# Attention's products turned by block reads and VectorE, and a three-pass rounding of the gate and up weights

## The chip, the cores and the metric

The kernel runs on one core of one Trainium2 chip. The metric is device time in microseconds (us) of one execution. A core has a matrix engine (TensorE, PE in the profile; its weight loads are PEld), VectorE (DVE), ScalarE (ACT), GpSimd (POOL), and SyncE (SP), which here only issues DMA transfers. Each engine takes its instructions in order; engines wait for one another by semaphores. On-chip data lies in SBUF (128 partitions), matmul results in PSUM.

## What is computed

One pre-norm block in float32 on x of shape 4 x 512 x 512: an attention of the Fourier kind, then a gated feed-forward whose weights are rounded to float8 (e4m3) values first.

```python
# attention on the layer-normed x; B=4, S=512, D=512, 16 heads of 32
q  = (x @ W_q.T ).reshape(B, S, H, hd)
kv = (x @ W_kv.T).reshape(B, S, H, hd)
qf  = l2_normalize(fft(q));  kvf = l2_normalize(fft(kv))
kvf = cumsum(kvf, axis=1)
values = ifft(qf * kvf).real.reshape(B, S, D)
x = x + values @ W_o.T
# feed-forward on the layer-normed x; I=1536
wq(w) = w.astype(float8_e4m3fn).astype(float32)
gate = silu((xn @ wq(gate_w)) * gate_scale)
up   = (xn @ wq(up_w)) * up_scale
x = x + ((gate * up) @ wq(down_w)) * down_scale
```

## The kernel before

**Tiling.** The 4 x 512 tokens are 16 chunks of 128 tokens, four to a batch entry. `x` comes in twice, plain (`load_x`) and turned (`load_xT`). The Fourier transform is folded into W_q and W_kv at the start (`fold_in`, `folded`), its inverse into W_o (`fold_out`).

**Order.** The schedule is written by hand: the order of the calls is the order on each engine. A pass `for i in range(2, N)` runs the rounds of attention. In round i chunk i is projected to its spectrum (`spectrum(i, 1)` for the keys, `spectrum(i, 0)` for the queries, eight matmuls' rows each), its squares are taken on ACT and summed on DVE (`squared`, `summed`), and `norms` raises them to -1/2 on POOL. Chunk i-1 is scaled on DVE (`k_scaled` with the carried row of the chunk before, split into `kh` by ACT and `kl` by `k_low`; `q_scaled`), summed along the tokens by two matmuls with a triangular matrix (`running`, tile `cum`), its last row is carried on (`carry`: ACT copies 32 rows to `end`, a DMA on ACT's queue takes one of them to `row`), and multiplied (`products` on DVE, `combined` on POOL). Chunk i-2 is turned by four PE transposes into PSUM and copied to `qvT` by ACT (`v_transpose`), and projected by W_o (`project`, tile `po`). Chunk i-3 gets its residual on DVE and goes to DRAM (`finish`, tensor `y_all`). `x_stats` and `x_row`, `x_center` take the mean of the next chunks' tokens out of x.

**Rounding of the weights.** 18 units of 128 x 1024 weights (two each of gate, up, down for each of three column or row blocks) are rounded to float8 values by `quant_abs` (ACT: |w| scaled down), `quant_step` (DVE: exponent mask; then an operation that makes a large value where the weight overflows, on ACT in the rounds, on POOL later), `quant_floor`, `quant_add` and `quant_sub` (DVE). These are cut into `parts`, and `next_parts(n)` issues the next n of them: at three places before the rounds, at up to three places of each round by the list `given` (42 parts), the other 27 in the first steps of the feed-forward.

**Feed-forward.** For each batch entry 12 steps of `inner` (16 matmuls `gu` of gate and up, then Silu on ACT, `f` and `fl` on DVE, `fh` on ACT) and `down` of the step before (eight matmuls `pd`). The normed tokens of entry 0 are turned by PE (`y_transpose`); those of entries 1 to 3 by `y_blocks`, which writes them to DRAM and reads them back in four DMAs of 32 x 32 blocks, and `y_turn`, which turns each block by one DVE transpose. `behind` and `between` place that work after the matmuls of a step.

**SP's queue** carries, in the order of the program, loads of x, xT and weights (`load_unit`, 1 MB each), stores of y, the loads of y for each batch entry (`load_y`), the blocks and the output.

Of the kernel before, what the change touches and what calls it, by code (L numbers as in the profile page):

```python
# [7 lines left out]
F32 = mybir.dt.float32  # L8
# [7 lines left out]
P = 128  # L16
# [5 lines left out]

E4M3_MIN_NORMAL = 2.0**-6
E4M3_OVERFLOW = 464.0
ROUNDER = 1.5 * 2.0**20
DOWN = 2.0**-40
HUGE = 2.0**127
# [3 lines left out]
def tile_fft_attention_then_fp8_ffn(  # L31
# [53 lines left out]

    chunks = [(b, c) for b in range(B) for c in range(TC)]
# [13 lines left out]
    def load_x(i):  # L100
        b, c = chunks[i]
        t = work.tile([P, D], F32, tag="x", name=f"x_{b}_{c}", bufs=6)
        nc.sync.dma_start(t, x[b, c * P : (c + 1) * P, :])
        xt[i] = t
# [23 lines left out]
    nc.gpsimd.memset(over, -E4M3_OVERFLOW * DOWN * HUGE)  # L128

# [11 lines left out]
    xn_all = dram.tile([B, TC, P, D], F32, name="xn_all")  # L141

# [53 lines left out]
    def quant_abs(u):  # L196
        k = units[u][3]
        w = staged[u][:, k : k + QH, :]
        a = work.tile([P, QH, D], F32, tag="qa", name=f"qa_{u}")
        nc.scalar.activation(a, w, AF.Abs, scale=DOWN)  # L200
        quant[u] = (w, a)

    def quant_step(u, in_rounds):
        w, a = quant[u]
        m = work.tile([P, QH, D], F32, tag="qm", name=f"qm_{u}")
        nc.vector.tensor_scalar(
            m.bitcast(I32), a.bitcast(I32), 0x7F800000, None, ALU.bitwise_and
        )
        if in_rounds:
            nc.scalar.activation(a, a, AF.Identity, scale=HUGE, bias=over)  # L210
        else:
            nc.gpsimd.tensor_scalar(a, a, -E4M3_OVERFLOW * DOWN, HUGE, ALU.add, ALU.mult)
        quant[u] = (w, a, m)

    def quant_floor(u):
        _, a, m = quant[u]
        nc.vector.scalar_tensor_tensor(m, a, E4M3_MIN_NORMAL * DOWN, m, ALU.max, ALU.max)  # L217

    def quant_add(u):
        w, a, m = quant[u]  # L220
        nc.vector.scalar_tensor_tensor(a, m, ROUNDER / DOWN, w, ALU.mult, ALU.add)  # L221

    def quant_sub(u):
        _, a, m = quant[u]
        nc.vector.scalar_tensor_tensor(units[u][0], m, -ROUNDER / DOWN, a, ALU.mult, ALU.add)
# [4 lines left out]
    for u in range(len(units)):  # L230
        parts += [(quant_floor, u), (quant_add, u)]
        if u + 1 < len(units):
            parts.append((quant_step, u + 1))
        parts.append((quant_sub, u))

    def next_parts(n, in_rounds=False):

        for f, u in parts[:n]:
            if f is quant_step:
                f(u, in_rounds)  # L240
                if in_rounds and units[u][3] == 0 and u + QH < U1:
                    load_unit(u + QH)
            else:
                f(u)
            if f is quant_add and u + 1 < len(units):
                quant_abs(u + 1)
        del parts[:n]


    def stats(src, name):  # L250

        less = work.tile([P, 1], F32, tag="less", name=f"less_{name}", bufs=4)
        rstd = work.tile([P, 1], F32, tag="dev", name=f"dev_{name}", bufs=6)
        each = work.tile([P, D], F32, tag="end", name=f"each_{name}", bufs=1)
        nc.scalar.activation(each, src, AF.Identity, accum_out=less)
        nc.scalar.activation(less, less, AF.Copy, scale=-1.0 / D)
        nc.scalar.activation(each, src, AF.Square, bias=less, accum_out=rstd)
        nc.scalar.activation(rstd, rstd, AF.Identity, scale=1.0 / D, bias=eps)
        nc.gpsimd.tensor_tensor(rstd, rstd, nhalf[:, 0:1], ALU.pow)
        return less, rstd  # L260
# [12 lines left out]

    def heads(t):
        return t.rearrange("p (h f) -> p h f", f=HD)


    st_x, rows, xns, pqs, sss, rns, qns, kns, carries, cums, qvs, qvTs, pos = (
        {} for _ in range(13)
    )  # L280

    def nm(i):
        return "%d_%d" % chunks[i]

    def x_stats(i):
        st_x[i] = stats(xt[i], nm(i))
# [20 lines left out]
    def squares(i, j):  # L307
        squared(i, j)
        summed(i, j)
# [59 lines left out]
    def products(i):  # L369

        qn, cum = qns.pop(i), cums.pop(i)
        qv = work.tile([P, D], F32, tag="qv", name=f"qv_{nm(i)}")
        cross = work.tile([P, D], F32, tag="cross", name=f"cross_{nm(i)}", bufs=1)
        qh, ch, xh = heads(qn), heads(cum), heads(cross)
        nc.vector.tensor_tensor(qv, qn, cum, ALU.mult)
        nc.vector.tensor_tensor(xh[:, :, :HK], qh[:, :, :HK], ch[:, :, HK:], ALU.mult)
        nc.vector.tensor_tensor(xh[:, :, HK:], qh[:, :, HK:], ch[:, :, :HK], ALU.mult)
        qvs[i] = (qv, cross)
# [9 lines left out]
    def v_transpose(i):  # L388
        pt = transpose(qvs.pop(i)[0], f"v{nm(i)}")
        qvTs[i] = work.tile([P, KC, P], F32, tag="qvT", name=f"qvT_{nm(i)}", bufs=1)  # L390
        nc.scalar.copy(qvTs[i], pt)
# [25 lines left out]

    def y_norm(b, c):
        xns["y", b, c] = normed(ys[b][:, c, :], st_y.pop((b, c)), f"f{b}_{c}")
# [11 lines left out]
    def y_blocks(b, c):  # L431

        nc.sync.dma_start(xn_all[b, c], xns.pop(("y", b, c)))
        src = xn_all[b, c].rearrange("(i t) (k j f) -> j t k i f", t=HD, j=P // HD, f=HD)
        z = work.tile([P, KC, P], F32, tag="x", name=f"z_{b}_{c}", bufs=6)
        for j in range(P // HD):
            nc.sync.dma_start(
                z[j * HD : (j + 1) * HD].rearrange("t k (i f) -> t k i f", f=HD), src[j]
            )
        xns["z", b, c] = z  # L440

    def y_turn(b, c):
        if c == 0:
            yhs[b] = big_tile(f"yh_{b}", F32R)
            yls[b] = big_tile(f"yl_{b}", F32R)
        z = xns.pop(("z", b, c))
        t = work.tile([P, KC, P], F32, tag="xT", name=f"t_{b}_{c}", bufs=3)
        nc.vector.transpose(t.rearrange("p k n -> p (k n)"), z.rearrange("p k n -> p (k n)"))
        s = slice(c * P, (c + 1) * P)
        hi, lo = yhs[b][:, :, s], yls[b][:, :, s]  # L450
        nc.scalar.copy(hi, t)
        nc.gpsimd.tensor_tensor(lo, t, hi.bitcast(F32), ALU.subtract)
# [5 lines left out]
    def inner(n, on_pe, between):  # L458
# [19 lines left out]
        nc.vector.scalar_tensor_tensor(f, pgu[1], gus[:, 1, m : m + 1], g, ALU.mult, ALU.mult)  # L478
        fh = work.tile([P, S], F32R, tag="kh", name=f"fh_{b}_{m}", bufs=3)
# [7 lines left out]
    def down(steps):  # L487
# [17 lines left out]
        if steps[-1] % MC == MC - 1:  # L505
            for c in range(TC):
                o = work.tile([P, D], F32, tag="x", name=f"o_{b}_{c}", bufs=6)
                nc.vector.tensor_tensor(o, pds[b][c], dsc, ALU.mult)  # L508
                add = nc.vector if b == B - 1 and c % 2 else nc.gpsimd
                add.tensor_tensor(o, o, ys[b][:, c, :], ALU.add)  # L510
                nc.sync.dma_start(out[b, c * P : (c + 1) * P, :], o)
# [49 lines left out]
    next_parts(1, True)  # L561
# [9 lines left out]
    squares(1, 1)  # L571
    norms(1, 1)
    x_row(2)
    x_center(2)
    q_scaled(0)
    products(0)
    combined(0)
    spectrum(1, 0)
    squares(1, 0)
    k_scaled(1)  # L580
    k_low(1)
    norms(1, 0)


    given = [4 if i in (2, 5, 7, 9, 11) else 3 for i in range(N - 3)] + [2, 2, 0]
    for i in range(2, N):
        spectrum(i, 1)
        if i == N - 6:
            load_y(0)
        at(load_xT, i + 2)  # L590
        if i > 2:
            k_scaled(i - 1)
            finish(i - 3)
        at(load_x, i + 2)
        if i > 2:
            k_low(i - 1)
        squared(i, 1)
        v_transpose(i - 2)
        if i == 2:
            x_stats(3)  # L600
        next_parts(given[i] // 3, True)
        if i > 2:
            q_scaled(i - 1)
        summed(i, 1)
        norms(i, 1)
        if i == 2:
            q_scaled(1)
# [10 lines left out]
        combined(i - 1)  # L618
        if i == N - 1:
            y_transpose(0, TC - 2)  # L620
            y_transpose(0, TC - 1)
# [6 lines left out]
        project(i - 2)  # L628
# [6 lines left out]
    for _, u in parts:  # L635
        if u not in staged:
            load_unit(u)
            if 1 not in ys:
                load_y(1)
    finish(N - 3)  # L640
# [4 lines left out]
    def on_pe(n, part):  # L645
        if part == 0 and n < 2:
            v_transpose(N - 2 + n)
            if n == 1:
                finish(N - 2)
        elif part == 1 and n == 0:  # L650
            running(N - 1)
            products(N - 1)
            combined(N - 1)
            project(N - 2, "tp")
# [5 lines left out]
    def behind(n):  # L660
        b, m = divmod(n, MC)
        if n == 1:
            project(N - 1, "tp")
            finish(N - 1)
# [10 lines left out]
        if b + 1 < B and 0 <= m - 3 < TC:  # L675
            y_stats(b + 1, m - 3)


    for n in range(STEPS + 1):
        if n < STEPS:  # L680
            inner(n, on_pe, between)
# [70 lines left out]
```

## Time and profile before

The unprofiled runs took 479.96, 481.14 and 481.37 us, with a median of 481.14. The profiled execution took 480.92; its span, from the first to the last instruction, is 479.1.

| | |
|---|---|
| median of the runs | 481.14 us |
| profiled execution, and its span | 480.92 us, 479.1 us |
| start to the first round (i = 2) on PE | 0 to 32.8 us |
| rounds 2 to 15 | 32.8 to 194.8 us |
| feed-forward, 48 steps | 194.8 to 473.4 us |
| granted TensorE clock | 0.999 |
| four PE transposes of a chunk's products | 0.27 us each, 64 in all |
| POOL's power, `rn` | 3.38 us each, 32 in all |
| bytes moved | 40.7 MB, mean 85 GB/s |

The rows of a timeline give start, duration, engine, line, operation, tiles and shapes, and in brackets the idle time before and what ended it. A row with a count (x8) merges as many instructions. The rows of a table of windows give for each stretch its length, the busy time (and count) of PE, PEld, DVE, ACT and POOL, the granted clock, the DMA engines' mean busy share and GB/s.

### The profile page before, as it was taken

To read this page: it belongs to the slowest core of one execution; us is meant where nothing else is said; L and a number is where in the kernel's file an instruction comes from. 1 tells how busy PE (TensorE), PEld (TensorE's weight loads), DVE (VectorE), ACT (ScalarE), POOL (GpSimd) and SP (SyncE) were. 2 spreads that over 40 slices of the span, in tenths; PEclk is the share of its full clock that TensorE was granted. 3 is DMA by queue.
4 is the path that set the end of the run, shared out by engine and by line. 5 is a ranking of instruction groups with operands and counts; after the bars stand their busy time and mean duration, and the time that the engine had idled before them with its cause. 6 is when DMAs were issued, how large, how long until landed. Compare 5 with 4: busy or idle time off the path is not lost.

```text
span 479.1 us, 5013 instructions
## 1 busy us (share of the span) xinstructions
PE 466.3 (97%) x1736; PEld 313.7 (65%) x1736; DVE 286.4 (60%) x399; ACT 214.9 (45%) x418; POOL 200.9 (42%) x134
## 2 busy tenths in 40 slices
PE   6999999999999999999999999999999999999995
PEld 5534454444444445568888888888888888888883
DVE  1558998888998787768898352333433332522225
ACT  3647475655646864315753325533226433222220
POOL 0257999987897986531332140122210021400002
PEclk9999999999999999999999999999999999999999
DMA  8920424342442101424241040430041420200002
GB/s 288 349 66 23 154 86 134 110 148 87 140 154 68 64 22 35 164 91 150 55 100 22 1 175 2 100 77 0 22 155 36 96 46 0 89 0 1 0 0 88
DMA packets 46152, 40.72 MB, mean 85 GB/s; under 512 B 27696, under 2 KB 28080, under 8 KB 46128
## 3 DMA queue, kind: packets, MB, share of 16 engines
q1 hardware_dynamic: 45744, 40.39, 26.9%
q8 instruction: 13, 0.21, 0.2%
q14 instruction: 11, 0.09, 0.1%
q10 hardware_dynamic: 384, 0.03, 0.1%
HBM read 28.85 MB, written 11.53 MB: 84 GB/s over the span
## 4 chain that ended last, share of the span: by engine, by line
PE 77%; DVE 8%; ACT 5%; POOL 4%; DMA 3%; issue 2%; SPq 0%; DVEq 0%; ACTq 0%
PE gu L465 37%; PE pd L498 19%; PE pq L302 12%; PE po L397 6%; POOL rn L323 3%; DMA row<-end 2%; PE pkv L150 1%; PE pt_v L271 1%; ACT sq L313 1%; ACT end L364 1%; DVE ss L318 1%; DVE qm L217 1%; PE pw L165 1%; PE cum L357 1%; DVE qa L221 1%
## 5 line engine op out<-in xcount | busy, mean ns | idle before, releaser
L323 POOL TENSOR_TENSOR rn<-ss,nhalf 128x16 f32<-128x16 f32 x32 | 108.2, 3383 | 22.5 <-DVE ss L318 22.5
L478 DVE SCALAR_TENSOR_TENSOR f<-gu,gus,g 128x512 f32<-128x512 f32 x48 | 36.0, 750 | 114.4 <-PE gu L465 112.9
L465 PE MATMUL gu<-yh,wg 128*128 128x512 f32 x192 | 77.0, 401 | 0.0
L465 PE MATMUL gu<-yh,wu 128*128 128x512 f32 x192 | 76.2, 397 | 0.0
L465 PE MATMUL gu<-yl,wg 128*128 128x512 f32 x192 | 75.8, 395 | 0.0
L498 PE MATMUL pd<-wd,fl 128*128 128x512 f32 x192 | 75.7, 394 | 0.0
L498 PE MATMUL pd<-wd,fh 128*128 128x512 f32 x192 | 75.7, 394 | 0.0
L465 PE MATMUL gu<-yl,wu 128*128 128x512 f32 x192 | 75.7, 394 | 0.0
L481 ACT CAST fh<-f 128x512 fp32r<-128x512 f32 x48 | 29.8, 621 | 90.8 <-DVE f L478 90.8
L302 PE MATMUL pq<-wkv,xT 128*128 128x512 f32 x128 | 57.7, 594 | 0.8 <-DVE xT L294 0.8
L476 ACT ACTIVATE g<-gu,gus 128x512 f32<-128x512 f32 x48 | 33.0, 688 | 55.2 <-PE gu L465 55.2
L397 PE MATMUL po<-wo,qvT 128*128 128x512 f32 x128 | 57.6, 593 | 0.0
L302 PE MATMUL pq<-wq,xT 128*128 128x512 f32 x128 | 57.6, 592 | 0.0
L510 POOL TENSOR_TENSOR o<-o,ys 128x512 f32<-128x512 f32 x14 | 17.7, 1295 | 83.6 <-DVE o L508 83.6
L483 DVE TENSOR_TENSOR fl<-f,fh 128x512 fp32r<-128x512 f32 x48 | 36.2, 755 | 27.0 <-ACT fh L481 26.8
L302 PEld LDWEIGHTS pq<-wkv,xT 128*128 128x128 f32 x128 | 24.1, 190 | 30.6 <-issue 27.5
L465 PEld LDWEIGHTS gu<-yh,wg 128*128 128x128 f32 x192 | 36.0, 188 | 9.3 <-issue 0.5
L465 PEld LDWEIGHTS gu<-yl,wg 128*128 128x128 f32 x192 | 36.0, 188 | 9.2 <-issue 0.5
L498 PEld LDWEIGHTS pd<-wd,fh 128*128 128x128 f32 x192 | 36.0, 188 | 8.9
L498 PEld LDWEIGHTS pd<-wd,fl 128*128 128x128 f32 x192 | 36.0, 188 | 8.8 <-DVE fl L483 0.2
L465 PEld LDWEIGHTS gu<-yl,wu 128*128 128x128 f32 x192 | 36.1, 188 | 8.7
L465 PEld LDWEIGHTS gu<-yh,wu 128*128 128x128 f32 x192 | 36.0, 188 | 8.5
(84 smaller groups left out, 596.4 us busy)
## 6 DMA issues: line engine op xcount, KB each, us to landing
x<-in_x SPq DMA_DIRECT2D x16, 256.0 KB, 2.8
xT<-in_xT SPq DMA_DIRECT2D x16, 256.0 KB, 2.6
y_all<-x SPq DMA_DIRECT2D x16, 256.0 KB, 2.0
ys<-y_all SPq DMA_DIRECT2D x4, 1024.0 KB, 6.8
out<-o SPq DMA_DIRECT2D x16, 256.0 KB, 2.0
rawf<-in_gate_w SPq DMA_DIRECT2D x3, 1024.0 KB, 6.9
rawf<-in_up_w SPq DMA_DIRECT2D x3, 1024.0 KB, 5.4
rawf<-in_down_w SPq DMA_DIRECT2D x3, 1024.0 KB, 6.2
```

The costliest lines, as they stand in the source:

```text
L150: nc.tensor.matmul(pw[i][:, j * P : (j + 1) * P], lhsT=r[:, j, i * P : (i + 1) * P], rhs=fwd, start=True, stop=True,)
L165: nc.tensor.matmul(pw, lhsT=inv, rhs=r[:, j, :], start=True, stop=True)
L302: nc.tensor.matmul(pq, lhsT=xTs[i][:, k, :], rhs=w[:, k, :], start=k == 0, stop=k == KC - 1)
L323: nc.gpsimd.tensor_tensor(rns[i, j], sss.pop((i, j)), nhalf, ALU.pow)
L397: nc.tensor.matmul(po, lhsT=qvT[:, k, :], rhs=wo[:, k, :], start=k == 0, stop=k == KC - 1)
L465: nc.tensor.matmul(p, lhsT=w[:, k, m * P : (m + 1) * P], rhs=v[:, k, :], start=k == 0 and v is yhs[b], stop=k == KC - 1 and v is yls[b],)
L476: nc.scalar.activation(g, pgu[0], AF.Silu, scale=gus[:, 0, m : m + 1])
L478: nc.vector.scalar_tensor_tensor(f, pgu[1], gus[:, 1, m : m + 1], g, ALU.mult, ALU.mult)
L481: nc.scalar.copy(fh, f)
L483: nc.vector.tensor_tensor(fl, f, fh.bitcast(F32), ALU.subtract)
L498: nc.tensor.matmul(pds[b][c], lhsT=v[:, c * P : (c + 1) * P], rhs=wd[:, m, :], start=m == 0 and v is fused[n][0], stop=m == MC - 1 and v i ...
L510: add.tensor_tensor(o, o, ys[b][:, c, :], ALU.add)
```

## The change

There are four parts.

1. The products `qv` are no longer turned by PE. `v_blocks` writes them to a DRAM tensor `qv_all` and reads them back in four block DMAs into `z`, all on SP's queue; `v_turn` turns the blocks with one DVE transpose into `qvT`. The helpers `blocks` and `turned` are shared with the feed-forward's `y_blocks` and `y_turn`.
2. The output projection comes a round later: round i now has `project(i - 3)`, then `v_turn(i - 2)`, and `finish(i - 4)`. Round 2 is written out ahead of the loop, which begins at 3. The last projections lie in the feed-forward's first steps. Seven x tiles for six.
3. Gate and up weights are rounded in three DVE passes: a mask that also sets a bit (`quant_step`), add, subtract. What the floor did is done by a column `c` of one number per row: ACT sums Relu of the scaled |w| beyond the overflow bound over the row, and a 128 x 1 operation makes of it the least rounder, or a huge one for a row with overflow. Down weights keep four passes. The list `given` falls to 2 or 3 a round (29 parts), six parts lie before, 25 in the feed-forward.
4. Smaller: the two half products into `cross` become one with a reversed stride; `stats` is cut into `mean` and `deviation` and writes to the tag `tmp` where it wrote to `end`; weight loads are noted in `wanted` and issued after `v_blocks`; the loads of the last weight units are spread over the feed-forward's first steps; the feed-forward's means are taken ahead of `fh` on ACT; `qv` has one buffer.

```diff
     def quant_abs(u):
+        _, src, _, k = units[u]
         w = staged[u][:, k : k + QH, :]
         a = work.tile([P, QH, D], F32, tag="qa", name=f"qa_{u}")
-        nc.scalar.activation(a, w, AF.Abs, scale=DOWN)
-        quant[u] = (w, a)
+        m = work.tile([P, QH, D], F32, tag="qm", name=f"qm_{u}")
+        c = None
+        if src is down_w:
+            nc.scalar.activation(a, w, AF.Abs, scale=DOWN)
+        else:
+            c = work.tile([P, 1], F32, tag="qc", name=f"qc_{u}")
+            nc.scalar.activation(a, w, AF.Abs, scale=UP)
+            nc.scalar.activation(m, a, AF.Relu, scale=FAR, bias=far, accum_out=c)
+            nc.scalar.activation(c, c, AF.Identity, scale=HUGE, bias=least)
+        quant[u] = (w, a, m, c)
     def quant_step(u, in_rounds):
+        if c is not None:
+            nc.vector.tensor_scalar(
+                m.bitcast(I32), a.bitcast(I32), 0x7F800000, 0x00400000, ALU.bitwise_and, ALU.bitwise_or
+            )
+            return
     def quant_add(u):
+        if c is not None:
+            nc.vector.scalar_tensor_tensor(a, m, c, w, ALU.max, ALU.add)
     def quant_sub(u):
+        if c is not None:
+            nc.vector.scalar_tensor_tensor(to, m, c, a, ALU.max, ALU.subtract, reverse1=True)
...
-        each = work.tile([P, D], F32, tag="end", name=f"each_{name}", bufs=1)
+        each = work.tile([P, D], F32, tag="tmp", name=f"each_{name}")
...
+    def blocks(z, there, tokens):
+        nc.sync.dma_start(there, tokens)
+        src = there.rearrange("(i t) (k j f) -> j t k i f", t=HD, j=P // HD, f=HD)
+        for j in range(P // HD):
+            nc.sync.dma_start(
+                z[j * HD : (j + 1) * HD].rearrange("t k (i f) -> t k i f", f=HD), src[j]
+            )
+    def turned(t, z):
+        nc.vector.transpose(t.rearrange("p k n -> p (k n)"), z.rearrange("p k n -> p (k n)"))
...
-        nc.vector.tensor_tensor(xh[:, :, :HK], qh[:, :, :HK], ch[:, :, HK:], ALU.mult)
-        nc.vector.tensor_tensor(xh[:, :, HK:], qh[:, :, HK:], ch[:, :, :HK], ALU.mult)
+        nc.vector.tensor_tensor(xh, qh, ch[:, :, ::-1, :], ALU.mult)
...
-    def v_transpose(i):
-        pt = transpose(qvs.pop(i)[0], f"v{nm(i)}")
+    def v_blocks(i):
+        zs[i] = work.tile([P, KC, P], F32, tag="z", name=f"zv_{nm(i)}", bufs=1)
+        blocks(zs[i], qv_all[i], qvs.pop(i)[0])
+    def v_turn(i):
         qvTs[i] = work.tile([P, KC, P], F32, tag="qvT", name=f"qvT_{nm(i)}", bufs=1)
-        nc.scalar.copy(qvTs[i], pt)
+        turned(qvTs[i], zs.pop(i))
...
+    load_xT(4)
+    load_x(4)
+    spectrum(2, 1)
+    squared(2, 1)
+    x_stats(3)
+    next_parts(1, True)
+    spectrum(2, 0)
+    x_row(3)
+    running(1)
+    squared(2, 0)
+    carry(1)
+    x_center(3)
+    summed(2, 1)
+    norms(2, 1)
+    q_scaled(1)
+    products(1)
+    combined(1)
+    v_blocks(1)
+    next_parts(1, True)
+    summed(2, 0)
+    norms(2, 0)
+    x_stats(4)
+    next_parts(1, True)
+    v_turn(0)
-    given = [4 if i in (2, 5, 7, 9, 11) else 3 for i in range(N - 3)] + [2, 2, 0]
-    for i in range(2, N):
+    given = [3 if i % 2 else 2 for i in range(N - 3)] + [2, 2, 0]
+    for i in range(3, N):
         spectrum(i, 1)
         at(load_xT, i + 2)
-            finish(i - 3)
+        at(finish, i - 4)
         at(load_x, i + 2)
         squared(i, 1)
-        v_transpose(i - 2)
...
         products(i - 1)
         combined(i - 1)
+        v_blocks(i - 1)
+        while wanted:
+            load_unit(wanted.pop())
...
-        project(i - 2)
+        project(i - 3)
+        v_turn(i - 2)
...
+    load_unit(U1)
+    load_y(1)
+    finish(N - 4)
...
     def on_pe(n, part):
-        if part == 0 and n < 2:
-            v_transpose(N - 2 + n)
-            if n == 1:
-                finish(N - 2)
-        elif part == 1 and n == 0:
+        if part == 1 and n == 0:
             running(N - 1)
             products(N - 1)
             combined(N - 1)
-            project(N - 2, "tp")
+            v_blocks(N - 1)
+            project(N - 3, "tp")
...
     def behind(n):
         if n == 1:
+            load_unit(U1 + QH)
+            finish(N - 3)
+            v_turn(N - 2)
+        elif n == 2:
+            project(N - 2, "tp")
+            v_turn(N - 1)
+        elif n == 3:
+            finish(N - 2)
             project(N - 1, "tp")
+            load_unit(U1 + 2 * QH)
+        elif n == 4:
             finish(N - 1)
```

## The prediction

> **What bounds the kernel now.** I read the busy shares, the chain that ended last, TensorE's (PE's) rows in order of time, a table of busy time by round, and then the other engines' rows in the same stretches.
>
> ```profile
> PE 466.3 (97%) x1736; PEld 313.7 (65%) x1736; DVE 286.4 (60%) x399; ACT 214.9 (45%) x418; POOL 200.9 (42%) x134
> ...
> PE 77%; DVE 8%; ACT 5%; POOL 4%; DMA 3%; issue 2%; SPq 0%; DVEq 0%; ACTq 0%
> ```
>
> PE is busy 97% of the span, but ends of matmuls are modelled, so the starts decide. One round of attention:
>
> ```profile
> 101.83 3.60 PE L302 MATMUL pq<-wkv,xT 128*128 128x512 f32 x8
> 105.26 0.60 PE L271 MATMUL pt_v<-tab,qv 128*128 128x128 f32 x4
> 105.70 3.60 PE L302 MATMUL pq<-wq,xT 128*128 128x512 f32 x8
> 109.14 0.27 PE L290 MATMUL row<-tab,less 128*128 128x128 f32 x1
> 109.16 0.48 PE L357 MATMUL cum<-kh,tri_r 128*128 128x512 f32 x1
> 109.48 0.40 PE L357 MATMUL cum<-kl,tri_r 128*128 128x512 f32 x1
> 109.72 3.60 PE L397 MATMUL po<-wo,qvT 128*128 128x512 f32 x8
> 113.15 3.60 PE L302 MATMUL pq<-wkv,xT 128*128 128x512 f32 x8
> ```
>
> The round starts at 101.83 and the next at 113.15, no row waits: 11.32 us of back-to-back work. The transposes cost the start of the next product less a plain product: (105.70 - 101.83) - (101.83 - 98.40) = 3.87 - 3.43 = 0.44. The feed-forward part is as dense: its steps come every 5.59 us (gu rows of the chain at 214.26, 219.85, 225.44), to 460. What the change does there beside PE is therefore free while fl comes within a step. So the rounds decide, and there the other engines are near PE (columns: PE, PEld, DVE, ACT, POOL busy):
>
> ```profile
> 75.92:87.24 11.32, 11.32 (x32) 5.39 (x32) 10.86 (x15) 6.97 (x14) 10.33 (x6) 1.00 0.25 76
> 87.24:98.56 11.32, 11.32 (x32) 5.38 (x32) 9.94 (x15) 6.01 (x13) 10.33 (x6) 1.00 0.44 151
> ...
> sum 113.40, PE 113.40 PEld 53.55 DVE 98.72 ACT 72.06 POOL 98.19; mean PE 11.34 PEld 5.35 DVE 9.87 ACT 7.21 POOL 9.82
> ```
>
> Over ten rounds VectorE (DVE) takes 9.87 and GpSimd (POOL) 9.82 of 11.34.
>
> **Part 1: transposes off PE.** Sixteen groups of four go: 14 in the rounds and 2 in the feed-forward's first steps (there 197.09 to 197.44 plus a slower next matmul, also about 0.44). 16 x 0.44 = **-7.0 us**. ScalarE (ACT) loses 16 copies of qvT at 0.58, off the path. One PE wait in front of a transpose goes as well, 0.59 at 186.54 (for DVE yl): **-0.6**.
>
> What takes their place, per chunk: a store on SP, four block reads on SP, one DVE transpose. Rows: t<-z transpose 0.70; the reads in the feed-forward: store issued at 232.26, first read at 235.16, four issues 2.71 together, last landing 2.5 after its issue. The last issue starts near 237.2, so z is there at 239.7: **7.5 us from store to z**. GpSimd ends combined() at 148.30 where the next round starts at 147.11, so z is there 1.2 + 7.5 = 8.7 us into that round. v_turn waits anyway until project() has read the one qvT buffer, at the round's end, 10.88. Cover: 2.2 us. If it is gone, DVE stands still, and behind v_turn stand k_scaled, finish, k_low, q_scaled and x_center, for which the next spectrum waits. SP's queue: per round 0.33 + 2.0 wait + 2.7 + xT 0.33 + y 0.33 + x 0.38 + at most one weight load 0.4 = 6.5 of 10.9, so x and xT come some 4 us later than now; both are wanted a round later (x by x_stats, xT by x_center), with landings of 2.8 and 2.6. No cost.
>
> A rule speaks against the reads: the Trainium skill, "DMA: Bandwidth & Descriptors", Specifications, wants 512 bytes or more per transfer, below which the engines read, modify and write; the blocks are read in 128-byte pieces. If each piece cost as one of 512, four reads would weigh like one 1 MB load, and by an estimate from that z would come some 4 to 5 us later, the case of rival 2; the trace's 2.5 us for 64 KB says no, though with less other traffic than the rounds have.
>
> **Part 2: DVE and ACT in a round.** DVE gains 0.70 (turn) and changes two cross products (0.33 apart each, 0.66) for one over 512 elements: nearest row qv, 0.60 apart; bounds 0.60 and 0.70, nothing. Gate and up units drop the floor pass (1.24). The two-operation mask, the max-with-column add and subtract are not in the trace: between their present rows (0.68, 1.22, 1.22) and those under GpSimd's shadow (1.22, 1.60, 1.72); I take the present. The rounds are given 2.5 parts each, 3.3 before: 0.8 x 1.17 = -0.95. DVE: 9.87 + 0.70 - 0.95 = **9.6 of 10.88**. ACT: per gate or up unit Relu with a sum (L210's 1.15 + 0.19) and one 128x1 row (0.30) for L210's 1.15: +0.5; minus 0.58 per round. And the step in which ACT waited for DVE (qa L210 <- qm, 14.0 us in all) goes for these units. POOL keeps its 9.82, 90% of a round: the thinnest cover. Its loop is rn(q) to q_scaled, ss, rn(k), two combined() rows, rn(q):
>
> ```profile
> 70.39 2.91 POOL L323 TENSOR_TENSOR rn<-ss,nhalf 128x16 f32<-128x16 f32 x1
> 73.26 0.56 POOL L259 TENSOR_TENSOR dev<-dev,nhalf 128x1 f32<-128x1 f32 x1
> 74.75 3.82 POOL L323 TENSOR_TENSOR rn<-ss,nhalf 128x16 f32<-128x16 f32 x1 [0.93 <-DVE ss L318]
> 78.54 0.70 POOL L385 TENSOR_TENSOR qv<-qv 128x240 f32<-128x240 f32 x1
> 79.31 1.03 POOL L386 TENSOR_TENSOR qv<-cross 128x240 f32<-128x240 f32 x1
> 80.31 3.88 POOL L323 TENSOR_TENSOR rn<-ss,nhalf 128x16 f32<-128x16 f32 x1
> ```
>
> From 70.39 to 80.31 that is 9.9 us; other turns take 10.3 to 11.8 (80.31 to 92.09), because the same operation takes 2.91 beside some DVE work and 3.88 beside other. The removed floor is such neighbour work; I take 10.4, under 10.88, cost nothing, and 11.3 as the far end (rival 1).
>
> **Part 3: the start.** Projection comes a round later, so PE has 3.43 us less to do while the first chunks pass DVE, ACT and POOL, and it waits for them. I walked rounds 2 to 4 with the rows' durations.
> - Gain: stats no longer write the tile end, so ACT does not wait for the row's DMA (13.8 us in five waits, the first 25.80 to 27.63), and x_center(2) stands ahead of summed(1,1). spectrum(2,1) starts at 31.8 for 32.79; PE waits of 0.31 and 0.39 go.
> - k_scaled(1) 36.0, kh 37.3, x_stats(3), row(3) 39.1, x_center(3) 40.1: round 3 starts on PE at 40.1 and its two spectra end at 47.0.
> - The squaring of x(3) now uses a tmp buffer that summed(2,1) must have read (40.7), so ACT reaches carry(1) at 42.6, products(1) ends at 44.4, then add, sum, step, turn to 47.5, k_scaled(2) with its row 48.8, kh 49.4, kl(2) **50.1**. cum(2) waits on PE from 47.2 to 50.1.
> - project(0) ends at 54.1; x_center(4), behind rn(2,0) at 51.2, at 54.3; round 4 starts at 54.4, round 5 at 65.4 without a wait (x_center(5) at 64.4).
>
> Before, round 5 started at 67.87. Without project's 3.43 and three transposes (1.3) that would be 63.1; I get 65.4: **+2.3 us**. Bounds: nothing, or the 3.43 that were moved.
>
> **Part 4: into the feed-forward.** cum(15) now waits 1.08 for the bank that ACT frees late, because kh waits for a row that took 6.1 us behind two 1 MB loads (issued at 189.41 and 190.64, the row at 191.96). These loads now stand behind v_blocks(14) on SP, so the row goes first (1.7): a wait of 0.3 is left, **-0.8**. The late projections (3 x 3.43) are the same work at another place. v_turn(14) stands about 13 us after the first gu row, z(14) is there at 7; for chunk 15 some 18 against 15 to 18 behind the 2 MB: no more than a DVE wait inside a step. Parts left: 25 for 27, three passes for most.
>
> **Sum**: span 479.1 - 7.0 - 0.6 + 2.3 - 0.8 = 473.0. The profiled run took 480.92, 1.8 above its span and 0.2 below the median of 481.14. 473.0 + 1.8 = 474.8, with the 0.2: **475.0**.
>
> **Rivals.** Differences under 0.3% (1.4 us) cannot be told from no change.
> 1. DVE, POOL and ACT set the round, which stays at 11.3: the 6.2 us of the 14 round transposes are not had, the rest is: 475.0 + 0.42 x 12 = **480**. For: POOL at 90%, loops of 10.3 to 11.8 now. Against: the floor and the ACT waits go. 20%.
> 2. The block reads come late in the rounds, which carry more traffic (150 GB/s in every other round against 60 in the feed-forward). The loop combined, store to z, turn, k_scaled to products, combined spans two rounds: z time + 0.6 + 7.4 + 0.6 + 2.1. With 21.8 for two rounds it decides from a z time of 11 us. With landings like the 1 MB loads (6.9 for 2.5) and 0.9 more on the store it is 12.8: 0.85 more a round, 11 rounds, **484**, slower. Against: x and xT land in 2.6 to 2.8 in the rounds. 11%.
> 3. Relu makes ACT load tables. The trace has one load of 1.28 for all its functions, and Relu is not among them. Two loads for each of 12 units are 31 us on ACT, 2.1 a round, on 7.3: it fits, but kh and the carry come 2.6 later in such rounds: about **479**. 3%. The Trainium skill, "ScalarE: Activation LUTs", Table sets, counts relu among the cheap functions that are in every set, so no load; no row here shows it.
>
> My forecast, PE setting the pace of nearly every round: 60%, 472.8 to 477.5. Another 6% for slower by something unnamed. Low end 472.8 (start free of cost); the high end reaches over rival 1 to 482.0, leaving out rival 2, the unnamed and a little below. Faster: 60 + 12 of rival 1 + 2 = 74%; same 9%; slower 17%.
>
> **What would show it.** Right: rounds 10.9 apart on PE from the fifth on, no pt_v rows, one PE wait near 2.9 at cum(2), one table load, feed-forward steps of 5.59. Wrong: rounds at 11.3 with PE waiting for x_center or cum (rival 1); DVE t<-z waiting for DMA (rival 2); or PE waits at project().

## The result, and the profile after

| | before | after |
|---|---|---|
| median of the runs | 480.97 us (479.96 to 481.37, 4 runs) | 489.09 us (488.21 to 489.91, 4 runs) |
| span of the profiled execution | 479.1 us | 486.8 us |
| round 5 begins on PE | 67.87 us | 64.72 us |
| feed-forward begins on PE | 194.81 us | 200.10 us |

The changed kernel takes 1.0172 times as long, with an interval of 1.0145 to 1.0198. It was forecast to be faster. The start is 3.2 us earlier than before, as it should be; between round 5 and the feed-forward everything is lost, and more.

The page of the kernel after: the busy shares, the chain that ended last, and the DMA issues with their median time to landing in the last column.

```profile
PE 465.5 (96%) x1672; PEld 308.6 (63%) x1672; DVE 276.8 (57%) x387; ACT 214.9 (44%) x429; POOL 191.4 (39%) x133
...
PE 63%; DVE 5%; ACT 4%; DMA 4%; issue 1%; SPq 1%; POOL 1%; DVEq 0%; ACTq 0%; POOLq 0%
...
x<-in_x SPq DMA_DIRECT2D x16, 256.0 KB, 4.9
xT<-in_xT SPq DMA_DIRECT2D x16, 256.0 KB, 4.7
qv_all<-qv SPq DMA_DIRECT2D x16, 256.0 KB, 2.0
zv<-qv_all SPq DMA_DIRECT2D x64, 64.0 KB, 2.5
```

PE has 64 instructions less (the transposes), but its share of the chain falls from 77% to 63%: it now waits for others. The block reads land in 2.5 us, as the row of the feed-forward promised; it is x and xT that land late, in 4.9 and 4.7 us where it was 2.8 and 2.6. The rows of the kernel before for these two, and for ACT's wait for x:

```profile
x<-in_x SPq DMA_DIRECT2D x16, 256.0 KB, 2.8
xT<-in_xT SPq DMA_DIRECT2D x16, 256.0 KB, 2.6
...
ACT each L255 <- DMA x<-in_x: 5.5, 2, 3.3
```

The waits of the kernel after (engine, line waited at, what ended the wait: total us, times, longest us) say whom that hits:

```profile
PE cum L413 <- ACT kh L399: 7.9, 7, 2.1
PE cum L413 <- DVE kl L404: 1.4, 6, 0.2
PE cum L413 <- ACT g L535: 0.3, 1, 0.3
...
ACT each L288 <- DMA x<-in_x: 32.3, 10, 6.8
...
ACT qa L215 <- DMA rawf<-in_down_w: 9.8, 2, 7.3
...
SPq L320 <- POOL qv L441: 71.1, 15, 6.8
SPq L323 <- DMA qv_all<-qv: 34.3, 16, 5.9
```

ACT waited for x 5.5 us in two waits before; now it is 32.3 us in ten. PE had no wait for kh before; now it has seven. SP stands 71.1 us at the block store for GpSimd's end of the products, and 34.3 us at the reads for the store to land. What follows on SP in the program waits too. A wait of the kind seen here, in PE's rows of two rounds (start, duration, and in brackets the idle time before and what ended it):

```profile
113.62 3.60 PE L358 MATMUL pq<-wkv,xT 128*128 128x512 f32 x8
...
120.49 0.27 PE L346 MATMUL row<-tab,less 128*128 128x128 f32 x1
120.52 0.48 PE L413 MATMUL cum<-kh,tri_r 128*128 128x512 f32 x1
120.84 0.40 PE L413 MATMUL cum<-kl,tri_r 128*128 128x512 f32 x1
...
124.50 3.60 PE L358 MATMUL pq<-wkv,xT 128*128 128x512 f32 x8
...
131.37 0.27 PE L346 MATMUL row<-tab,less 128*128 128x128 f32 x1
132.61 0.50 PE L413 MATMUL cum<-kh,tri_r 128*128 128x512 f32 x1 [0.96 <-ACT kh L399]
133.33 0.50 PE L413 MATMUL cum<-kl,tri_r 128*128 128x512 f32 x1 [0.23 <-DVE kl L404]
...
137.10 1.45 PE L358 MATMUL pq<-wkv,xT 128*128 128x512 f32 x3
```

The first of these rounds takes 124.50 - 113.62 = 10.88 us, exactly what was forecast. The second takes 137.10 - 124.50 = 12.60. A listed wait of 0.96 cost 1.72: kh starts 1.24 after row instead of 0.03, and kl 0.72 after kh instead of 0.32, because it is made of kh. Now ACT beside it, and below it SP, on which each row is the issue of a transfer:

```profile
123.17 0.50 ACTq L422 DMA_DIRECT2D row<-end  x1
129.92 0.63 ACT L288 ACTIVATE each<-x 128x512 f32<-128x512 f32 x1 [6.77 <-DMA x<-in_x]
...
131.95 0.60 ACT L399 CAST kh<-kn 128x512 fp32r<-128x512 f32 x1
```

```profile
106.88 0.33 SPq L320 DMA_DIRECT2D qv_all<-qv  x1
108.94 2.61 SPq L323 DMA_DIRECT2D zv<-qv_all  x4
111.64 0.57 SPq L105 DMA_DIRECT2D xT<-in_xT  x1
112.31 0.38 SPq L464 DMA_DIRECT2D y_all<-x  x1
112.74 0.42 SPq L110 DMA_DIRECT2D x<-in_x  x1
117.11 0.33 SPq L320 DMA_DIRECT2D qv_all<-qv  x1
119.17 2.60 SPq L323 DMA_DIRECT2D zv<-qv_all  x4
121.87 0.57 SPq L205 DMA_DIRECT2D rawf<-in_up_w  x1
122.54 0.45 SPq L105 DMA_DIRECT2D xT<-in_xT  x1
123.04 0.42 SPq L464 DMA_DIRECT2D y_all<-x  x1
123.51 0.67 SPq L110 DMA_DIRECT2D x<-in_x  x1
```

Read the last row first. The x load at 123.51 belongs to the round that began at 113.62; it stands behind the store, the 2 us wait for its landing, the four reads, a 1 MB load of weights, xT and y. ACT wants that x from 123.2 on, for `x_stats(i + 2)`, which is the last of the same round. It gets it at 129.92. `kh` of the next round stands behind `x_stats` on ACT, so it starts at 131.95, and PE waits. One round earlier there was no weight load in front: x was issued at 112.74, landed in 3.3 us and not in 6.3, ACT waited 5.70 us for it, and PE did not wait. What decides is not the length of ACT's wait but when `x_stats` begins: 116.19 is 2.57 us into the next round and early enough for that round's `kh`, 129.92 is 5.42 us into it and too late. In the kernel before, SP's row for x is this:

```profile
105.95 0.38 SPq L103 DMA_DIRECT2D x<-in_x  x1
```

Its round began at 101.83, so x was issued 4.12 us into it. After, it is 112.74 - 102.64 = 10.10 us into the round. Of the ten rounds from 64.72 to 188.86 in the kernel after, four take 10.87 to 10.98 us and six take 12.30 to 15.95. In the four, `x_stats` begins 0.6 to 2.6 us into the round, in the six 4.9 to 6.2 us into it. In three of the six ACT waits last for an x behind a 1 MB load (of weights twice, of y once), in two for a load of down weights and then for x, and in the last, round 14, for DVE (run 5 shows this wait).

### The profile page after: what moved, and what is told of

It reads as the page before. It is cut to its first block, busy times and chain, and to the rows that moved or that the text cites. A ratio compares the mean times of both kernels' runs of the same rounds, so it can differ in the third digit from the quotient of the medians.

```text
span 486.8 us, 5056 instructions
## 1 busy us (share of the span) xinstructions
PE 465.5 (96%) x1672; PEld 308.6 (63%) x1672; DVE 276.8 (57%) x387; ACT 214.9 (44%) x429; POOL 191.4 (39%) x133
## 2 busy tenths in 40 slices
DMA packets 82250, 49.13 MB, mean 101 GB/s; under 512 B 61744, under 2 KB 62128, under 8 KB 82224
## 4 chain that ended last, share of the span: by engine, by line
PE 63%; DVE 5%; ACT 4%; DMA 4%; issue 1%; SPq 1%; POOL 1%; DVEq 0%; ACTq 0%; POOLq 0%
PE gu L524 36%; PE pd L558 18%; PE po L455 4%; DMA x<-in_x 3%; PE pq L358 3%; ACT kh L399 1%; PE cum L413 1%; ACT sq L369 1%; SPq L323 1%; ACT each L296 1%; DVE qa L245 0%; DVE ss L374 0%; ACT each L288 0%; DVE kl L404 0%; DVE kn L396 0%
## 5 line engine op out<-in xcount | busy, mean ns | idle before, releaser
L379 POOL TENSOR_TENSOR rn<-ss,nhalf 128x16 f32<-128x16 f32 x32 | 105.0, 3281 | 25.8 <-DVE ss L374 25.8
L524 PE MATMUL gu<-yh,wg 128*128 128x512 f32 x192 | 78.0, 406 | 0.0
L455 PE MATMUL po<-wo,qvT 128*128 128x512 f32 x128 | 58.6, 601 | 0.0
L358 PEld LDWEIGHTS pq<-wq,xT 128*128 128x128 f32 x128 | 24.2, 190 | 30.4 <-issue 30.1
L298 POOL TENSOR_TENSOR dev_f<-dev_f,nhalf 128x1 f32<-128x1 f32 x16 | 10.3, 646 | 84.6 <-ACT dev_f L297 84.5
```

What stands on the lines that cost most here:

```text
L358: nc.tensor.matmul(pq, lhsT=xTs[i][:, k, :], rhs=w[:, k, :], start=k == 0, stop=k == KC - 1)
L379: nc.gpsimd.tensor_tensor(rns[i, j], sss.pop((i, j)), nhalf, ALU.pow)
L455: nc.tensor.matmul(po, lhsT=qvT[:, k, :], rhs=wo[:, k, :], start=k == 0, stop=k == KC - 1)
L524: nc.tensor.matmul(p, lhsT=w[:, k, m * P : (m + 1) * P], rhs=v[:, k, :], start=k == 0 and v is yhs[b], stop=k == KC - 1 and v is yls[b],)
```

## The experiments

The theory: x and the weights come late because of their place on SP behind the block store and reads; the transposition by blocks itself, the three-pass rounding and the later projection do what was forecast. Rivals: the block traffic (49.13 MB for 40.7) slows the other transfers wherever they stand; or another part of the change costs the time. Runs 1 to 4 were made together, 5 to 8, and 9 to 11; the median of the kernel before beside them is 480.7 us for the first two groups and 481.0 for the third.

**1. x a round earlier.** The carried row stays in its tile to make room for an eighth x tile.

```diff
-    XB = 7
+    XB = 8
...
-            row = work.tile([1, D], F32, tag="row", name=f"row_{nm(i)}", bufs=1)
+            row = end[:1, :]
...
+    load_x(5)
...
-        at(load_x, i + 2)
+        at(load_x, i + 3)
```

> The changed kernel, with each x chunk loaded one round earlier (eight x tiles; the carried row is kept in the first partition of the tile it comes from, to make room). Theory A (SP's queue: the x load stands behind the block reads and weight loads, ACT waits for it and takes kh late, PE waits at cum): ACT's waits for x fall from 32.3 us to under 3, the PE waits for kh from 7.9 us to under 2, rounds 10.9 us apart; 475 to 479 us. Rival B (the block reads' traffic slows every transfer): the waits move to the weight loads and the carried row, 483 to 488. Rival C (the loop of GpSimd, VectorE and ScalarE sets the round at 11.3 or more): ACT no longer waits for x, PE still waits at cum, 482 to 487.

481.07 us (480.16 to 482.22); against the kernel before 1.0009 [0.9996, 1.0022]. 8 us of the loss are gone, though not one byte moves less: it is the time of x that cost them. The gain falls 2 us short of theory A's range, though rounds 6 to 12 are 10.88 us each. The waits of this kernel:

```profile
PE cum L413 <- ACT kh L399: 4.2, 4, 2.1
...
ACT qa L215 <- DMA rawf<-in_down_w: 11.5, 2, 7.2
ACT each L288 <- DMA x<-in_x: 6.5, 3, 3.7
```

x is awaited about as little as before the change (6.5 us for 5.5). What is left are two waits of ACT for down weights, which also stand behind the reads on SP; `kh` is again queued behind them. Half of PE's 4.2 us, the longest wait, is in round 14.

**2. Weight loads behind x.** They are issued after x's load of the next round instead of straight after the reads.

```diff
         at(load_x, i + 2)
+        while wanted:
+            load_unit(wanted.pop())
         k_low(i - 1)
...
         v_blocks(i - 1)
-        while wanted:
-            load_unit(wanted.pop())
```

> The changed kernel, with the 1 MB weight loads issued behind the next round's x load instead of ahead of it. Theory A: in the four or five rounds that load weights x lands in about 4.5 us for 6.5 and about 2 us earlier; each such round gets 1 to 2 us shorter, 481 to 486; more waits of ACT for the weights take a part back. Rivals B and C: no gain, 487 to 490.

480.86 us (479.41 to 482.5); 1.0003 [0.9986, 1.0021]. x is issued about 1 us earlier (8.99 us into a round for 10.10) and lands without a 1 MB load in front, in 3.7 us (median) for 4.9:

```profile
PE cum L413 <- ACT kh L399: 4.3, 3, 2.2
...
ACT each L288 <- DMA x<-in_x: 28.6, 10, 4.6
```

ACT still waits 28.6 us in ten waits, but the longest is 4.6 where it was 6.8, and most of PE's waits are gone: rounds 5 to 13, from 69.25 to 167.32, take 10.86 to 11.04 us each, with `x_stats` beginning 0.8 to 3.9 us into them. So the late place of x alone costs these rounds nothing; it did so together with a 1 MB load in front. And the sum of ACT's waits is no measure of the loss; what counts is how many of them make `kh` late. What is left is lost in round 14 and in round 4, which takes 15.08: the carried row, issued 1.9 us after a load of weights, lands in 6.7 us there, and the clock falls (last section). The time lies just under theory A's range.

**3. Turned by PE again,** with the rest of the change.

```diff
     def v_blocks(i):
-        zs[i] = work.tile([P, KC, P], F32, tag="z", name=f"zv_{nm(i)}", bufs=1)
-        blocks(zs[i], qv_all[i], qvs.pop(i)[0])
+        pass
     def v_turn(i):
+        pt = transpose(qvs.pop(i)[0], f"v{nm(i)}")
...
-        turned(qvTs[i], zs.pop(i))
+        nc.scalar.copy(qvTs[i], pt)
```

> The changed kernel, with the products turned by TensorE again (no store, no block reads; one buffer more for qv), the later projection and the three-pass rounding kept. Theory A: without the block reads SP is free, x lands in time, rounds 11.3 us apart: 480 to 483, the level of the kernel before. Rival B: the same. Rival C: no change from the changed kernel's 489, as the vector work is nearly the same.

481.24 us (480.85 to 485.58); 1.0026 [1.0005, 1.0047]. Without the block DMAs the loss is gone, and rounds 5 to 13 are 11.30 to 11.31 us, which rules out rival C. The other parts of the change together are worth about nothing here.

**4. x issued by ACT,** in the same round as in the changed kernel.

```diff
-        at(load_x, i + 2)
         k_low(i - 1)
         squared(i, 1)
+        at(load_x, i + 2, nc.scalar)
```

> The changed kernel, with the x loads of the rounds issued on ScalarE's queue (0.4 to 0.5 us of ACT each), so that they pass by SP's queue but share the same 16 engines. Theory A: x is issued early in its round, ACT's wait for it falls under 5 us in all, 475 to 480. Rival B: x is issued early but lands as late, 485 to 489. Rival C: ACT does not wait, PE does, 482 to 487.

480.56 us (478.0 to 481.15); 0.9988 [0.9971, 1.0005]. The block traffic is all there, x goes to the same DMA engines, and its eleven loads from ACT land in 2.8 us as before the change. Rounds 6 to 13 take 10.88 to 10.95 us. The rival of traffic falls as the cause: it is the place on SP, with what stands in front there. (xT, which stays behind the reads on SP, still lands in 4.3 us.) The time is 0.6 us above theory A's range. The Trainium skill, "DMA: Bandwidth & Descriptors", "Issuing engines are not separate DMA queues", says that starting DMAs from several engines only saves the time that a sequencer takes to initiate them, usually small beside the DMA itself. The saving here was larger, 489.09 - 480.56 = 8.5 us, and of another kind: issuing an x takes SP 0.42 us, but in the kernel after SP's sequencer stood, in all, 71.1 and 34.3 us in waits ahead of its loads.

**5. x a round earlier and weights ahead of the block store** (run 1 with the weight loads moved).

```diff
+        while wanted:
+            load_unit(wanted.pop())
         v_blocks(i - 1)
         if i == N - 6:
             load_y(0)
-        while wanted:
-            load_unit(wanted.pop())
```

> e1 (x a round earlier) with the round's weight load issued ahead of the block reads instead of behind them. e1's trace leaves three stalls, and in each ACT waits for a weight load (7.2 and 4.3 us) that stands behind the block reads on SP, or is still late from it. Theory A (only the order on SP costs): these waits fall under 1 us each, the PE waits for kh from 4.2 to about 0.3, every round from the fifth to the fourteenth 10.9 us: 474 to 477, faster than the kernel before by about 1%. Rival B (traffic): the weights land no earlier, or the block reads land later and VectorE waits: 480 to 484. Rival C (ScalarE's own load in the rounds with the feed-forward's means): two stalls of 1 to 3 us stay there, 477 to 479.

478.01 us (476.23 to 481.1); 0.9945 [0.9924, 0.9965]: 11 us under the changed kernel, and faster than the kernel before. It is 1 us above theory A and in the range of rival C, whose cause is there too, in one round for its two. Nine rounds from 65.99 to 163.91 are 10.88 us each. Of PE's waits for kh 1.2 us are left (its waits, and below them ACT's rows in round 14):

```profile
PE cum L413 <- ACT kh L399: 1.2, 2, 0.8
```

Round 14 still takes 13.33. ACT takes the means of the feed-forward's tokens in it, and DVE makes their `xn_f`; `each` waits for that, `kh` comes late again:

```profile
167.58 0.63 ACT L288 ACTIVATE each<-x 128x512 f32<-128x512 f32 x1 [2.65 <-DVE xn_f L308]
...
171.20 0.62 ACT L399 CAST kh<-kn 128x512 fp32r<-128x512 f32 x1 [1.43 <-DVE kn L396]
```

**6. The weights early alone** (x as in the changed kernel).

> The changed kernel with only the weight loads issued ahead of the block reads; x as in the changed kernel. Theory A: the weights no longer stand in front of x nor come late themselves; ACT's waits for x stay near 4 us each, within its slack, 477 to 481. If x alone were the cause, 485 to 489. Rival B: 485 to 489.

484.94 us (483.36 to 485.47); 1.0080 [1.0062, 1.0099]. ACT's waits for the down weights go, but those for x stay (38.4 us in 12, longest 6.9), and PE's for kh are 5.0 us in four. That is above theory A's range. The load of weights now delays the block store behind it: in the round from 110.75 the store is issued at 114.25 and the first read at 119.60, 5.35 us later for 2.06 elsewhere, and x, behind the reads, goes out 12.65 us into the round. Either half is worth less than both: 489.1 to 484.9 by the weights alone, to 481.1 by x alone, to 478.0 by both. The price of the weights alone is not a clean one: in the profiled execution the clock falls twice (last section), which makes two rounds 14.79 and 16.38 us long where rounds with waits of the same length took 13.31 (kernel after) and 14.60 (run 1), some 3 us together.

**7. Four DVE passes for all weights,** on run 5, with three or four parts a round for two or three.

```diff
-        if src is down_w:
+        if True:
...
-        if units[u][1] is down_w:
-            parts.append((quant_floor, u))
+        parts.append((quant_floor, u))
...
-    given = [3 if i % 2 else 2 for i in range(N - 3)] + [2, 2, 0]
+    given = [4 if i % 4 == 3 else 3 for i in range(N - 3)] + [2, 2, 0]
```

> e5 with all units rounded in four VectorE passes, as in the kernel before, 37 parts in the looped rounds for 29 (6 before them in both). Theory A (PE sets the pace, VectorE has room): VectorE rises to some 10.5 of 10.9 us in a round, a stall in some rounds: 476 to 480, 1 to 4 above e5. If the third pass did not matter: within 1 us of e5. If VectorE set the pace: rounds at 11.3 and more, 481 to 486.

485.01 us (484.8 to 485.52); 1.0088 [1.0074, 1.0103], 7 us more than run 5, for the 1 to 4 of theory A. With the turn on DVE as well, ACT waits for DVE's mask 21.7 us in nine waits (4.3 in two in run 5), and PE for kh 6.3 us. Of the 7.6 us between the spans, 2.7 are lost ahead of round 5, 2.0 in rounds 5 to 13, and 3.7 in round 14, where the clock falls too; the rest is small. So the first part needs the third beside it. Whether the fuller DVE or ACT's waits for the mask cost the time was not told apart; the rounds' slack is smaller than busy shares make it look.

**8. The kernel before again,** as a look at the level of the feed-forward.

> The kernel before, unchanged, for a profile beside the others on this chip: feed-forward steps of 5.595 us as in its first profile if the changed kernel's 5.61 is its own, 5.61 if it is the chip's or the profile's.

481.59 us, span 479.8. The steps are 5.594 us, so the changed kernel's 5.61 is its own. Between 250 and 400 us PE has 645 matmuls in the kernel before, in both profiles, and 643 in the kernel after and in every run made from it (642 in run 7).

**9. Run 5 with the products turned by PE** (the edits of runs 5 and 3 together), to price the first part where nothing is late; **10. x on ACT's queue and weights early** (the edits of runs 4 and 6), and **11. the kernel of run 5 again**, all on one chip.

> e5_x_and_weights_early with one thing undone: attention's products are turned by PE and copied by ACT again, without block reads. It prices Part 1 where x and the weights come early. Theory: 7.0 us more than e5 by the prediction's 16 x 0.44, less what e5 still loses in its last round, so 483 to 486, rounds 11.3 apart. Rival (the block reads gave nothing in the end, what they freed on PE is lost to waits): within 1.5 us of e5, 477 to 479.5.

> e4_x_on_act_queue (x loaded for the same round, but issued by ACT) with the weight loads issued ahead of the block store and reads, as in e5. If it is only SP's order that makes x and the weights late, taking x off SP and the weights ahead of the reads is as good as loading a round earlier: 477 to 479.5. If weight loads ahead of x make x's transfer itself slow (the 1 MB stands in front of it in the DMA engines), x is late again and the time is 481 to 485.

> The kernel of e5_x_and_weights_early again, beside the two others on one chip: 476 to 479.5 if its gain over the kernel before is real; 480 to 481 if it was that batch's luck.

| | median (lowest to highest) | against before | span | feed-forward begins |
|---|---|---|---|---|
| 9 | 480.96 (479.94 to 481.93) | 1.0001 [0.9989, 1.0013] | 478.8 | 192.16 |
| 10 | 476.51 (475.68 to 476.77) | 0.9909 [0.9891, 0.9927] | 475.0 | 188.31 |
| 11 | 476.91 (476.19 to 479.45) | 0.9915 [0.9892, 0.9939] | 477.7 | 191.00 |

The gain of run 5 comes again, and run 10 has it without an eighth x tile and with the row as the change has it: the two orders agree. Run 10 is 0.5 us better than expected. Run 9 misses its 483 to 486 by 2 us, and so falls between its theory and the rival: turning on DVE is worth 480.96 - 476.51 = 4.45 us to run 10, or 4.05 to run 11, not 7.0 and not nothing. The rows say where the rest went. From round 5 to the feed-forward run 9 takes 192.16 - 65.62 = 126.54 us and run 10 188.31 - 65.13 = 123.18, so 3.4 less. The rounds are 11.31 apart in the one and 10.88 in the other, but round 14 takes 12.77 (167.40 to 180.17) in the one and 13.38 (163.04 to 176.42) in the other, and in run 10 PE waits for kh there and gives the gain back. In the feed-forward the last transposes cost nearly nothing that shows: from the first gu row to the last pd row it is 280.84 us with them and 280.83 without, of which 0.26 is a wait for cum that only run 10 has.

## Why the prediction was wrong

**The step that failed** is the one on SP's queue: "x and xT come some 4 us later than now; both are wanted a round later (x by x_stats, xT by x_center), with landings of 2.8 and 2.6. No cost." It has three faults. x is not wanted a round later: `load_x(i + 2)` and `x_stats(i + 2)` are in the same round, the one early on SP, the other last on ACT. It came 6 us later and not 4 (10.10 us into the round for 4.12, in the rounds shown), because the store ahead of it waits for GpSimd's products and goes out 3.1 to 4.7 us into rounds 5 to 14, where 1.2 was put. And the landing was taken from the kernel before, where in the rounds no 1 MB load went out right in front of it; it became 4.9, and 6.3 behind such a load. Run 2 shows what this fault adds: late in place but with no such load in front, x held up no round from 5 to 13. The weight loads themselves, which moved behind the reads too, were counted as a term of the queue and not asked who waits for them; ACT waited 9.8 us for two of them. The cost is the difference to the run with both put right: from round 5 to round 15 the kernel after takes 124.14 us and run 10 111.29, so **12.9 us**, for a step entered at nothing; some 1.35 of it is a fall of the clock, told at the end. Of the 12.9, 2.6 lie in round 14. No rival named the step; the second named lateness from the reads, but of z. The prediction left 6% for something unnamed.

**What held.** PE setting the pace: undisturbed rounds are 10.88 apart, in the kernel after and in the others, so rival 1 (11.3) is out. The block reads: landing 2.5, and DVE has no wait for z in the profile after (one of 1.2 us in run 5), so the cover that rival 2 doubted held and its mechanism is out, although it alone forecast a slower kernel. DVE was put at 9.6 us of a round and took 9.1 (82.30 in the nine rounds from 65.13 of run 10). Relu: one table load in the profile after, as before, so rival 3 is out. The start: rounds 3, 4 and 5 were put at 40.1, 54.4 and 65.4 and began at 41.14, 53.75 and 64.72. Part of that is luck: the wait near 2.9 at cum(2), one of the signs, did not come (0.40 for kh and 0.23 for kl there), but row(3) and x_center(3) came later than put. PE's waits at cum, named as a sign of rival 1, came from late x and weights. cum(15) waits 0.3, as forecast. The three passes cost nothing in the rounds, and run 7 shows that four would.

**What was mis-sized.** Part 1's 7.0 measured 3.8 by the spans of runs 9 and 10. Rounds 5 to 13 gave 3.9 (101.78 less 97.91), as counted. The start, where transposes lie beside waits, gave 0.5 for the 1.3 of three groups; the feed-forward gave nothing for 0.9; rounds 14 and 15 took 0.5 back where 0.9 was counted. In round 14 ACT and DVE are so full that PE loses 1.6 us (13.38 less 10.88 and less the 0.87 of the two transposes of y); the kernel before lost 0.4 there already (12.60 less 11.32 and 0.87), so 1.2 is new. The feed-forward's step was taken as unchanged: it went from 5.592 to 5.614 us (seven steps from 237.97 to 277.27), 0.022 x 48 = 1.1.

So the sum closes. The forecast is 473.0. Add 12.9 for late x and weights and 1.2 for round 14; take off 0.7 for an earlier round 5 and 0.2 for a shorter round 15 (11.24 for 12.46 less 0.44 and 0.6); and add 0.7 for the feed-forward, 286.7 us for 286.0 (284.3 before, less 0.88 and 0.8, and 3.43 for the projection that moved there), its longer steps included. That is 486.9 for a span of 486.8. In run 10 the 12.9 go, the start is 0.3 early, round 14 costs the same 1.2, round 15 0.5 and the feed-forward 0.7: 475.1 for a span of 475.0.

**Open.** Why every matmul of the feed-forward stands some 0.4% further from the next is not settled. It is the same in run 9, so it is not the block DMAs of attention.

## What to carry over

When a store that waits for a slow engine, and reads that wait for that store, are put on a queue, everything behind them on that queue is issued late by these waits: list each transfer behind them with its consumer, the consumer's place on its engine, and what is queued behind that consumer. Take the landing of a transfer with what is now issued in front of it: here a late place alone stayed within the slack (run 2), and a place behind 1 MB did not. Then load a round earlier, or put the dependent chain and the plain loads on different issuing engines: here either turned a loss of 1.7% into a gain of 0.6 to 0.9%, once the weight loads too were taken from behind the reads.

## What the runs showed of the chip

Two waits of PE of the same length had different prices. In the kernel after, PE idles 2.10 us ahead of cum in round 14, and the granted clock (the column after PE's busy time) falls for about 4 us:

```profile
180.00:182.00 2.00, 0.05 (x1) 1.00 0.21 33
182.00:184.00 2.00, 1.85 (x3) 0.56 0.56 89
184.00:186.00 2.00, 2.00 (x4) 0.59 0.42 141
186.00:188.00 2.00, 2.00 (x7) 1.00 0.04 8
```

In run 1 the same wait of 2.10 us is at 172.34 to 174.44, and the clock stays:

```profile
172.00:174.00 2.00, 0.34 (x2) 1.00 0.10 16
174.00:176.00 2.00, 1.33 (x4) 1.00 0.54 84
176.00:178.00 2.00, 2.00 (x6) 1.00 0.57 164
```

The round takes 15.95 us in the one and 14.60 in the other, so the drop cost some 1.35 us. It is no single case. In windows of 1 us the clock falls to 0.50, and each time the windows add up to 3.4 us at half clock: once in the kernel after, once in run 2 (behind a wait for kh of 1.70 us), twice in run 6 (1.36 and 2.17) and once in run 7 (2.82). Waits of 1.36 in the kernel after, 2.09 in run 4 and 2.16 in run 2 were followed by no drop. The mean clock of the ten executions of run 1 goes from 0.993 to 1.000, so it differs between executions of one kernel too, and differences of 1 to 2 us between runs may hold some of it. What decides between them was not tried. The Trainium skill, "TensorE: Matmul & The Clock Gate", Part 1, puts the halved clock after an idle window of about 3.4 us; here waits of 1.4 to 2.8 us were sometimes enough.
